# Attention and graph attention on one core: adding two key tiles' weights ahead of the row-sum matmuls between two layers 1

## The chip, the cores and the metric

The kernel runs on one core of one Trainium2 chip. The metric is the device time of that core in microseconds; "the time" is a median of several runs. The engines of the core are TensorE (PE, its weight loads are shown as PEld), VectorE (DVE), ScalarE (ACT), GpSimd (POOL) and SyncE (SP, which issues the DMA transfers). Each works through its own queue of instructions, and they meet through semaphores.

## What is computed

The input is x of 8 batches, 2048 nodes and 256 features in fp32, with one adjacency matrix of 2048 x 2048. Layer 0 is an attention whose softmax is taken over each chunk of 256 keys by itself; the results of the 8 chunks are added. Layer 1 is a graph attention with one score per pair of nodes. Both end in a residual sum and a layer norm.

```python
# layer 0: H = 4 heads of 64, Nc = 8 chunks of 256 keys
scores = einsum('bhnd,bhjcd->bhnjc', q, kc) / sqrt(64)
scores = clip(scores, -10, 10)
scores = where(mask == 0, -10, scores)
attn = softmax(scores, axis=-1)              # over the 256 keys of a chunk
ctx = einsum('bhnjc,bhjcd->bhnd', attn, vc)  # added over the chunks
out = layernorm(ctx @ Wo.T + bo + x) * gamma + beta
x = layernorm(x + out)
# layer 1
e = leaky_relu(s_i[:, :, None] + s_j[:, None, :], 0.2)
attention = softmax(where(mask, e, -inf), axis=-1)
x = layernorm(x + elu(attention @ Wh))
```

## The kernel before

Every order of work is written out by hand. The outer loop goes over `J`, one step for each batch, block of 512 queries and chunk of 256 keys (8 x 4 x 8 = 256 steps). A step has two halves; a half is a *beat* and handles one tile of 128 keys. So layer 0 has 512 beats. In a beat PE makes the scores of four heads in two tiles of PSUM (L899), DVE clips and masks each (L909), and ACT takes the exponential of each into a tile `e` (L912). A chunk leaves four `e` tiles: two key tiles by two pairs of heads.

While chunk J is scored, the chunk before it (`prev`) is multiplied (L922 to L934). There are three passes: part 0 and part 1 are the two halves of each head's 64 features with `v` as weights, and part 2 has a matrix of ones as weights, which gives the softmax sums. Each pass has 2 key tiles x 4 heads = 8 matmuls (16 instructions in the profile), and each head fills 32 of the 128 output rows. The even beat runs parts 2 and 0, the odd beat part 1. ACT copies parts 0 and 1 into `un` (L936) and the sums into `ds` (L942). SP then moves the sums into a small tile `dc` (L944), DVE takes the reciprocal (L950), SP writes it to DRAM (`rd`, L952) and loads it spread over the rows (`r`, L956). Two beats after the sums DVE scales `un` (L963, or L961 for the first chunk), and POOL adds it to `ctxT` (L964). The functions `inverse`, `spread` and `scaled` are put on an `agenda` by the beat in which they are due, and `end_beat` runs them after the generators.

The generators advance by one step in each beat, inside `end_beat`. `fin` is the tail of a layer 0 block: x load, output projection (L357), statistics (L316), the multiplication by gamma and the sum with x (L370, L371), transposes and the store. `prelude` prepares layer 1 of a batch: it makes Wh (L398), key columns and rows, and, for every tile of queries, the maximum over two halves of the keys (`half_max`, L438), then `less_max` and `query_rows`. For the first query block the first four pairs of half maxima take two per beat. `layer1` yields the steps of layer 1: ACT makes the low branch (L714), DVE the leaky maximum (L718) and the mask (L723), ACT the exponential (L727), POOL the running sum (L736), PE the product (L746). `blocks_done` counts finished blocks of layer 1.

Layer 1 of a batch overlaps layer 0 of the next one. Between the last product of one batch's layer 1 and the first step of the next there is a stretch with layer 0, `fin` and `prelude` alone: beats 64 to 88, 134 to 152, 198 to 216 and so on, seven in all. The tiles that the change needs come from the pool `five`, tag `w` (five buffers), which layer 1 uses at other times (L713). The `e` tiles have eight buffers, `ps_m` has two.

Of the kernel before, what the change touches and what calls it, by code (L numbers as in the profile page):

```python
# [19 lines left out]
P = 128  # L20
# [8 lines left out]
def tile_adj_attention__then__gat(  # L29
# [312 lines left out]
    def fin(b, ib, ctxT):  # L342


        xt = one.tile([P, TPB, F], F32, tag="x", name=f"x{b}_{ib}")
        nc.sync.dma_start(out=xt, in_=x[b, ts(ib, IB), :].rearrange("(t p) f -> p t f", p=P))
        yield
        y = one.tile([P, TPB, F], F32, tag="y", name=f"y{b}_{ib}")
        nc.gpsimd.tensor_add(y, xt, bc_rows(bo_bc))  # L349
        nc.gpsimd.tensor_add(xt, xt, bc_rows(beta_bc))  # L350
        while (b, ib) not in ctx_done or ctx_done[b, ib] == beat:
            yield
        for t2 in range(TPB // 2):
            po = ps_m.tile([P, 2, F], F32, tag="m", name=f"po{b}_{ib}_{t2}")
            for j in range(2):
                for k in range(KC):
                    nc.tensor.matmul(  # L357
                        po[:, j, :],
                        ctxT[:, k, ts(2 * t2 + j, P)],
                        WT["o"][:, k, :],  # L360
                        start=(k == 0),
                        stop=(k == KC - 1),
                    )
            nc.vector.tensor_add(y[:, ts(t2, 2), :], po, y[:, ts(t2, 2), :])
        mv, rstd = yield from stats(y, f"a{b}_{ib}")
        yield
        normalize(y, mv, rstd, f"a{b}_{ib}")
        yield
        engine = nc.vector if (b, ib) == (B - 1, NIB - 1) else nc.gpsimd
        engine.tensor_mul(y, y, bc_rows(gamma_bc))  # L370
        engine.tensor_add(y, y, xt)  # L371
        yield
        mv, rstd = yield from stats(y, f"b{b}_{ib}")
        yield
        normalize(y, mv, rstd, f"b{b}_{ib}")
        nc.sync.dma_start(out=h_d[b, ib], in_=y)
        fin_near[b] += 1
        yield
        hT = four.tile([P, KC, IB], F32, tag="xT", name=f"hT{b}_{ib}")
        for k in range(KC):  # L380
            pt = ps_m.tile([P, TPB, P], F32, tag="m", name=f"pt{b}_{ib}_{k}")
            for t in range(TPB):
                nc.tensor.transpose(pt[:, t, :], y[:, t, ts(k, P)], ident)
            nc.scalar.copy(hT[:, k, :], pt.rearrange("p t c -> p (t c)"))
        if (b, ib) == (B - 1, NIB - 1):
            states[b]["hT"] = hT
        else:
            nc.sync.dma_start(out=hT_d[b, ib], in_=hT)
# [70 lines left out]
    def query_rows(m2, name):  # L459
        pt = ps_m.tile([2 * TPB, P], F32, tag="m", name=f"pab{name}")  # L460
        nc.tensor.transpose(pt, m2.rearrange("p n t -> p (n t)"), ident)
        rows = two.tile([2 * TPB, P], F32, tag="rows", name=f"abr{name}")
        nc.scalar.copy(rows, pt)
        ab_d = dram3.tile([2 * TPB, P], F32, tag="ab_d", name=f"ab_d{name}")
        nc.sync.dma_start(out=ab_d, in_=rows)
        return ab_d

    def query_bc(ab_d, name):
        ab = two.tile([P, 2, IB], F32, tag="ab", name=f"ab{name}")
        nc.sync.dma_start(  # L470
            out=ab.rearrange("p n q -> p (n q)"), in_=ab_d.rearrange("r c -> (r c)").partition_broadcast(P)
        )
        return ab

    def prelude(b):


        st = states[b]
        while fin_near[b] < NIB:
            yield  # L480
        hts = [load_hT(b, ib) for ib in range(2)]
        yield
        yield
        while blocks_done < b * NIB:
            yield
        wh = one.tile([P, NT, F + 2], F32, tag="wh", name=f"wh{b}")
        for ib in range(NIB):
            wh_block(b, wh[:, ts(ib, TPB), :], hts[ib], ib)
            if len(hts) < NIB:
                hts.append(load_hT(b, len(hts)))  # L490
            yield
        sj = two.tile([P, 3, NT], F32, tag="sj", name=f"sj{b}")
        key_columns(wh, sj, slice(0, NT))
        yield
        sj_row = one.tile([P, N], F32, tag="sj_row", name=f"sj_row{b}")
        key_rows(b, sj, sj_row, slice(0, NT))
        st["wh"], st["sj"] = [wh[:, ts(ib, TPB), :] for ib in range(NIB)], sj
        fbs, fb_load = far_loads(b, [(it, hf) for it in range(NT) for hf in range(2)])
        yield
        yield  # L500
        for ib in range(NIB):
            m2 = two.tile([P, 2, TPB], F32, tag="m2", name=f"m2{b}_{ib}")
            for n in range(2 * TPB):
                half_max(sj_row[:, ts(n % 2, HN)], fbs.pop(0), m2[:, n % 2, n // 2 : n // 2 + 1])
                fb_load()
                if ib or n % 2:
                    yield
            less_max(sj, ib, m2, f"{b}_{ib}")
            yield
            ab_d = query_rows(m2, f"{b}_{ib}")  # L510
            yield

            while blocks_done < b * NIB + ib - 1:
                yield
            st["ab"][ib] = (beat + 2, query_bc(ab_d, f"{b}_{ib}"))

    def last_prelude(b):

# [291 lines left out]
    def l1_open():  # L810
        return lows or edged or weighted

    def at(when, fn):
        agenda.setdefault(when, []).append(fn)

# [57 lines left out]
    for J in range(total + 1):  # L873
# [5 lines left out]
        for half in range(2):  # L879
# [37 lines left out]
            if prev is not None:  # L917
                if half == 0:

                    pool, tag = (one, "hr") if early and J % 3 == 2 else (two, "un")  # L920
                    prev["un"] = pool.tile([P, 2, IB], F32, tag=tag, name=f"un{prev['name']}")
                for part in ((2, 0), (1,))[half]:  # L922
                    m = ps_m.tile([P, IB], F32, tag="m", name=f"u{prev['name']}_{part}")
                    for i in range(2):
                        pc = 2 * prev["j"] + i
                        for h in range(H):
                            f0 = h * D + part * DH
                            nc.tensor.matmul(  # L928
                                m[h * DH : (h + 1) * DH, :],
                                prev["v"][pc // TPB][:, pc % TPB, f0 : f0 + DH] if part < 2 else ones[:, 0:DH],  # L930
                                prev["es"][2 * i + h // 2][:, h % 2, :],
                                start=(i == 0),
                                stop=(i == 1),
                            )  # L934
                    if part < 2:
                        nc.scalar.copy(prev["un"][:, part, :], m)  # L936
# [36 lines left out]
                        at(beat + 2 + 2 * lag, scaled)  # L973

            end_beat()
            if half == 1:

                if live and j == NCH - 2 and J + 2 < total:
                    nb, nib = (b, ib + 1) if ib + 1 < NIB else (b + 1, 0)
                    xq = xT_tile(nb, nib, "q")  # L980
                if live and j == NCH - 1 and J + 1 < total:
                    qT = make_qT(nb, nib, xq)
# [52 lines left out]
```

## Time and profile before

| what | us |
|---|---|
| median of 3 runs | 4392.91 (4389.68 to 4397.17) |
| the profiled execution's own time | 4387.29 |
| its span, first to last instruction | 4385.5 |
| PE busy | 4064.2 (93%) |
| DVE busy | 3417.7 (78%) |
| ACT busy | 2564.4 (58%) |
| POOL busy | 1760.5 (40%) |

The mean granted clock of TensorE is 0.98. In the lines of the profile, a group has the line of the kernel, the engine, the operation, the tiles as output<-input, partitions x elements, how often it ran, then busy us, mean ns of one, and the idle time of the engine just ahead of it with what ended it. A line of waits has who waited for whom, the total in us, how often, and the longest. A line of the timeline has the start, the length, and what ran; the idle time ahead of it stands in brackets. A line of stretches has start:end and length in us, busy us of each engine with its number of instructions, the granted clock, the busy share of the DMA engines, and GB/s. PE's ends are modelled, and matmuls overlap, so that starts are safer to read than lengths.

### The profile page before, as it was taken

How to read it: one execution, taken by the hardware profiler on the slowest of the kernel's cores; microseconds unless marked ns; L12 is line 12 of the kernel's file. 1: busy time of each engine (PE TensorE's matmuls, PEld its weight loads, DVE VectorE, ACT ScalarE, POOL GpSimd, SP SyncE). 2: the span in 40 equal slices, each digit the busy share in tenths (PEclk: the TensorE clock that was granted, in tenths of full speed). 3: DMA queues.
4: the chain of work that ended last, by engine and by line, in shares of the span. 5: the costliest groups of instructions: out<-in, count | busy, mean ns of one | idle time of the engine just before them, and what ended most of it. 6: DMA issues, size and time to landing. Idle time of an engine off the chain costs nothing. (4 is left out here: it accounts for less than half of the span.)

```text
span 4385.5 us, 61171 instructions
## 1 busy us (share of the span) xinstructions
PE 4064.2 (93%) x23053; PEld 1907.6 (43%) x23053; DVE 3417.7 (78%) x4530; ACT 2564.4 (58%) x3842; POOL 1760.5 (40%) x901
## 2 busy tenths in 40 slices
PE   8889989999999999999899999999999999899767
PEld 3223334454344534454344543445434454344456
DVE  5876589965998669976699766996579965888777
ACT  5655556665566556666566665566556665555546
POOL 0222235543455334444245442554325542354420
PEclk9999999999999999999999999999999999999889
DMA  5554232222332233321333223232232222322321
GB/s 166 182 163 149 71 115 86 83 73 89 99 90 81 64 107 102 100 75 51 105 102 98 74 74 105 85 95 78 70 106 85 89 78 67 115 83 80 123 73 58
DMA packets 257641, 415.63 MB, mean 95 GB/s; under 512 B 85440, under 2 KB 120512, under 8 KB 256448
## 3 DMA queue, kind: packets, MB, share of 16 engines
q1 hardware_dynamic: 257344, 411.71, 30.5%
q8 instruction: 181, 2.97, 0.3%
q14 instruction: 116, 0.95, 0.1%
HBM read 340.66 MB, written 68.88 MB: 93 GB/s over the span
## 5 line engine op out<-in xcount | busy, mean ns | idle before, releaser
L912 ACT ACTIVATE e<-sc 128x1024 f32<-128x1024 f32 x1024 | 1034.2, 1020 | 1049.9 <-DVE sc L909 1006.7
L909 DVE SCALAR_TENSOR_TENSOR sc<-sc,mk 128x1024 f32<-128x1024 f32 x1024 | 1206.7, 1223 | 538.3 <-PE sc L899 352.6
L899 PE MATMUL sc<-qT,kT 64*128 64x512 f32 x4096 | 1060.4, 633 | 86.7 <-ACT e L912 86.2
L964 POOL TENSOR_TENSOR ctxT<-ctxT,un 128x1024 f32<-128x1024 f32 x224 | 568.5, 2538 | 1145.3 <-DVE un L963 1007.0
L928 PE MATMUL u<-e,v 128*32 128x512 f32 x8192 | 980.9, 597 | 0.0
L746 PE MATMUL us<-wh,w 128*128 128x256 f32 x3584 | 878.6, 395 | 81.9 <-ACT w L727 60.4
L746 PEld LDWEIGHTS us<-wh,w 128*128 128x128 f32 x3584 | 667.7, 193 | 422.2 <-ACT w L727 110.7
L736 POOL TENSOR_TENSOR acc<-acc,w 128x512 f32<-128x512 f32 x392 | 601.7, 1535 | 544.9 <-ACT w L727 534.4
L899 PEld LDWEIGHTS sc<-qT,kT 64*128 64x128 f32 x4096 | 347.2, 189 | 611.6 <-ACT e L912 281.8
L718 DVE SCALAR_TENSOR_TENSOR w<-ab,sj,w 128x512 f32<-128x512 f32 x512 | 571.5, 1137 | 4.6 <-ACT w L714 4.5
L928 PEld LDWEIGHTS u<-e,v 128*32 128x32 f32 x8192 | 240.6, 110 | 659.7 <-issue 543.9
L928 PE MATMUL u<-e,ones 128*32 128x512 f32 x4096 | 497.5, 604 | 0.0
L723 DVE TENSOR_TENSOR w<-w,mk 128x512 f32<-128x512 f32 x512 | 458.6, 917 | 37.1 <-DMA mk<-mask 34.6
L438 DVE CUSTOM_DVE_ANT_0 fb<-sj_row,fb 128x1024 bf16<-128x1024 f32 x240 | 387.8, 1626 | 2.3 <-DMA fb<-far 2.3
L714 ACT ACTIVATE w<-ab,sj 128x512 f32<-128x512 f32 x512 | 352.2, 714 | 8.7 <-POOL acc L734 5.4
L727 ACT ACTIVATE w<-w 128x512 f32<-128x512 f32 x512 | 308.8, 629 | 75.9 <-DVE w L723 75.3
L936 ACT COPY un<-u 128x512 f32<-128x512 f32 x512 | 300.5, 587 | 66.5 <-PE u L928 57.6
L963 DVE TENSOR_TENSOR un<-un,r 128x1024 f32<-128x1024 f32 x224 | 278.1, 1242 | 42.2 <-DMA r<-rd 36.7
L928 PEld LDWEIGHTS u<-e,ones 128*32 128x32 f32 x4096 | 107.8, 110 | 356.5 <-issue 305.4
L950 DVE RECIPROCAL dc<-dc 128x16 f32<-128x16 f32 x256 | 63.9, 249 | 149.8 <-DMA dc<-ds 134.0
L942 ACT COPY ds<-u 128x512 f32<-128x512 f32 x256 | 148.5, 580 | 3.0 <-PE u L928 2.5
L349 POOL TENSOR_TENSOR y<-x,bo_bc 128x1024 f32<-128x1024 f32 x32 | 77.6, 2426 | 163.6 <-DMA x<-in_x_dram 103.0
(112 smaller groups left out, 3114.7 us busy)
## 6 DMA issues: line engine op xcount, KB each, us to landing
r<-rd SPq DMA_DIRECT2D x256, 256.0 KB
mk<-mask SPq DMA_DIRECT2D x120, 512.0 KB
fb<-far SPq DMA_DIRECT2D x240, 256.0 KB
xT_k<-in_xT_dram SPq DMA_DIRECT2D x32, 512.0 KB
raw<-in_adjT_dram SPq DMA_DIRECT2D x32, 512.0 KB
rawf<-in_adj_dram SPq DMA_DIRECT2D x32, 512.0 KB
x<-in_x_dram SPq DMA_DIRECT2D x32, 512.0 KB
h_d<-y SPq DMA_DIRECT2D x32, 512.0 KB
```

The source lines that it names most:

```text
L438: nc.vector.tensor_tensor_reduce(out=fb, in0=row, in1=fb, scale=1.0, scalar=2 * FAR * 0.999, op0=ALU.add, op1=ALU.max, accum_out=dst,)
L714: nc.scalar.activation(self.w, k["ab"][:, 1, :], AF.Identity, bias=k["sj"][:, 1, c : c + 1])
L718: nc.vector.scalar_tensor_tensor(self.w, k["ab"][:, 0, :], k["sj"][:, 0, c : c + 1], self.w, ALU.add, ALU.max)
L723: nc.vector.tensor_tensor(self.w, self.w, self.k["mks"][self.c // HT][:, self.c % HT, :], ALU.min)
L727: nc.scalar.activation(self.w, self.w, AF.Exp)
L736: nc.gpsimd.tensor_add(k["acc"], k["acc"], self.w)
L746: nc.tensor.matmul(k["us"][:, t, :], self.w[:, ts(t, P)], k["wh"][c // TPB][:, c % TPB, 0:F], start=(first and t % 2 == 0), stop=last, ski ...
L899: nc.tensor.matmul(sc[:, h, :], kTs[b][c // TPB][h * D : (h + 1) * D, hp, ts(c % TPB, P)], qT[h * D : (h + 1) * D, hp, :], start=True, sto ...
L909: nc.vector.scalar_tensor_tensor(scs[hp], scs[hp], -CLIP, cap, ALU.max, ALU.min)
L912: nc.scalar.activation(e, scs[hp], AF.Exp)
L928: nc.tensor.matmul(m[h * DH : (h + 1) * DH, :], prev["v"][pc // TPB][:, pc % TPB, f0 : f0 + DH] if part < 2 else ones[:, 0:DH], prev["es"] ...
L964: nc.gpsimd.tensor_add(p["ctxT"], p["ctxT"], p["un"])
```

## The change

In the seven stretches, the exponentials of a chunk's two key tiles are added before the sums' matmuls. A new function `l1_rests` says whether layer 1 rests: no step of it is open, its last batch is done, and the prelude of the next batch has not yet sent the rows of its first query block (it sets `near` then). When a chunk's second beat ends and layer 1 rests, POOL adds the two key tiles of heads 0 and 1 (`add_weights(nc.gpsimd, cur, 0)`), each 128 x 512 in fp32; a beat later DVE does the same for heads 2 and 3. For such a chunk, the pass of sums uses the four sums instead of the eight exponentials, so it has 4 matmuls instead of 8, and it stands in the odd beat ahead of part 1, with part 0 alone in the even beat. What follows the sums (copy, transfers, reciprocal, scaling, sum into `ctxT`) comes a beat later with it. In a `fin` block whose L370 and L371 fall into such a stretch, these two run on DVE instead of POOL. The first query block of a batch's layer 1 starts a beat later if its start would be even.

```diff
--- before.py
+++ after.py
@@ -366,7 +366,7 @@
         yield
         normalize(y, mv, rstd, f"a{b}_{ib}")
         yield
-        engine = nc.vector if (b, ib) == (B - 1, NIB - 1) else nc.gpsimd
+        engine = nc.vector if (b, ib) == (B - 1, NIB - 1) or l1_rests() else nc.gpsimd
         engine.tensor_mul(y, y, bc_rows(gamma_bc))
         engine.tensor_add(y, y, xt)
         yield
@@ -508,11 +508,14 @@
             less_max(sj, ib, m2, f"{b}_{ib}")
             yield
             ab_d = query_rows(m2, f"{b}_{ib}")
+            st["near"] = True
             yield
 
             while blocks_done < b * NIB + ib - 1:
                 yield
-            st["ab"][ib] = (beat + 2, query_bc(ab_d, f"{b}_{ib}"))
+
+            start = beat + 2
+            st["ab"][ib] = (start + (ib == 0 and start % 2 == 0), query_bc(ab_d, f"{b}_{ib}"))
 
     def last_prelude(b):
 
@@ -809,6 +812,19 @@
 
     def l1_open():
         return lows or edged or weighted
+
+    def l1_rests():
+
+        if not 2 * NIB * NCH <= beat < 2 * total or l1_open() or leaking:
+            return False
+        return blocks_done % NIB == 0 and "near" not in states[blocks_done // NIB]
+
+    def add_weights(engine, chunk, hp):
+
+        for h in range(2):
+            w2 = five.tile([P, IB], F32, tag="w", name=f"w2{chunk['name']}_{hp}_{h}")
+            engine.tensor_add(w2, chunk["es"][hp][:, h, :], chunk["es"][2 + hp][:, h, :])
+            chunk["w2"].append(w2)
 
     def at(when, fn):
         agenda.setdefault(when, []).append(fn)
@@ -919,18 +935,20 @@
 
                     pool, tag = (one, "hr") if early and J % 3 == 2 else (two, "un")
                     prev["un"] = pool.tile([P, 2, IB], F32, tag=tag, name=f"un{prev['name']}")
-                for part in ((2, 0), (1,))[half]:
+                added = prev.get("w2")
+                for part in (((0,), (2, 1)) if added else ((2, 0), (1,)))[half]:
                     m = ps_m.tile([P, IB], F32, tag="m", name=f"u{prev['name']}_{part}")
-                    for i in range(2):
+                    summed = part == 2 and added
+                    for i in range(1 if summed else 2):
                         pc = 2 * prev["j"] + i
                         for h in range(H):
                             f0 = h * D + part * DH
                             nc.tensor.matmul(
                                 m[h * DH : (h + 1) * DH, :],
                                 prev["v"][pc // TPB][:, pc % TPB, f0 : f0 + DH] if part < 2 else ones[:, 0:DH],
-                                prev["es"][2 * i + h // 2][:, h % 2, :],
+                                added[h] if summed else prev["es"][2 * i + h // 2][:, h % 2, :],
                                 start=(i == 0),
-                                stop=(i == 1),
+                                stop=(i == 1 or bool(summed)),
                             )
                     if part < 2:
                         nc.scalar.copy(prev["un"][:, part, :], m)
@@ -973,6 +991,11 @@
                         at(beat + 2 + 2 * lag, scaled)
 
             end_beat()
+            if prev is not None and half == 0 and "w2" in prev:
+                add_weights(nc.vector, prev, 1)
+            if live and half == 1 and l1_rests():
+                cur["w2"] = []
+                add_weights(nc.gpsimd, cur, 0)
             if half == 1:
 
                 if live and j == NCH - 2 and J + 2 < total:
```

## The prediction

> **What bounds the kernel now.** I read the page's busy shares first, then its groups, then stretches, waits and timeline of one pause between two layers 1. Busy shares and groups:
>
> ```profile
> PE 4064.2 (93%) x23053; PEld 1907.6 (43%) x23053; DVE 3417.7 (78%) x4530; ACT 2564.4 (58%) x3842; POOL 1760.5 (40%) x901
> ...
> L909 DVE SCALAR_TENSOR_TENSOR sc<-sc,mk 128x1024 f32<-128x1024 f32 x1024 | 1206.7, 1223 | 538.3 <-PE sc L899 352.6
> ...
> L736 POOL TENSOR_TENSOR acc<-acc,w 128x512 f32<-128x512 f32 x392 | 601.7, 1535 | 544.9 <-ACT w L727 534.4
> ...
> L438 DVE CUSTOM_DVE_ANT_0 fb<-sj_row,fb 128x1024 bf16<-128x1024 f32 x240 | 387.8, 1626 | 2.3 <-DMA fb<-far 2.3
> ...
> L928 PE MATMUL u<-e,ones 128*32 128x512 f32 x4096 | 497.5, 604 | 0.0
> ```
>
> PE at 93% makes a saved matmul look like saved time. But a share is an average; the change acts in seven pauses only. So, a pause (beats 262 to 279) in three stretches; columns are length, then busy us of PE, PEld, DVE, ACT, POOL:
>
> ```profile
> 2065.60:2087.40 21.80, 20.90 (x147) 7.18 (x146) 17.88 (x34) 17.11 (x26) 13.58 (x7) 1.00 0.37 120
> 2087.40:2138.30 50.90, 47.11 (x269) 21.27 (x265) 18.44 (x21) 26.60 (x45) 7.06 (x3) 1.00 0.28 85
> 2138.30:2189.60 51.30, 43.98 (x275) 14.75 (x274) 44.25 (x67) 23.64 (x32) 20.58 (x9) 0.97 0.34 109
> ```
>
> The middle stretch, where Wh (L398) is made, is PE's: DVE works 18 of 51 us. The last, with the half maxima (L438), is DVE's: 44 of 51 us, and its 7 idle us are waits on DMA, PE and POOL. The waits and the timeline (start, us) show two couplings:
>
> ```profile
> DVE dc L950 <- DMA dc<-ds: 134.0, 98, 4.7
> ```
> ```profile
> 2139.54 2.36 DVE L909 SCALAR_TENSOR_TENSOR sc<-sc,mk 128x1024 f32<-128x1024 f32 x2 [6.45 <-ACT qT L257]
> 2145.40 0.25 DVE L950 RECIPROCAL dc<-dc 128x16 f32<-128x16 f32 x1 [2.38 <-DMA dc<-ds]
> 2145.57 2.34 DVE L909 SCALAR_TENSOR_TENSOR sc<-sc,mk 128x1024 f32<-128x1024 f32 x2
> 2147.82 1.22 DVE L438 CUSTOM_DVE_ANT_0 fb<-sj_row,fb 128x1024 bf16<-128x1024 f32 x1
> 2148.95 3.38 DVE L438 CUSTOM_DVE_ANT_0 fb<-sj_row,fb 128x1024 bf16<-128x1024 f32 x1
> ```
> ```profile
> 2140.22 1.93 PE L928 MATMUL u<-e,ones 128*32 128x512 f32 x16
> 2141.96 1.90 PE L928 MATMUL u<-e,v 128*32 128x512 f32 x16
> 2143.79 1.99 PE L899 MATMUL sc<-qT,kT 64*128 64x512 f32 x8
> ```
> ```profile
> 2147.87 3.38 POOL L350 TENSOR_TENSOR x<-x,beta_bc 128x1024 f32<-128x1024 f32 x1
> 2151.21 3.35 POOL L964 TENSOR_TENSOR ctxT<-ctxT,un 128x1024 f32<-128x1024 f32 x1
> ```
>
> First: after the sums, the reciprocal waits for a DMA round trip and ends 6.0 us after that beat's clip began (2139.54 to 2145.57); the next clip stands behind it, though PE had begun the next scores at 2143.79. Second: a half maximum that takes 1.22 us alone took 3.38 with a GpSimd operation beside it, which itself took 3.38.
>
> [...] The clip has one operand in PSUM and shows no such stretching (1223 ns). [...] the trace has 0.69 us for 128x512 adds (L364), and 0.60 from start to start. [...] the trace's 1.27 is used. [...]
>
> **The change, part by part.** By the built order, it takes in 65 chunks (11 in the first pause, 9 in each of six). Layer 1 starts in the same beats as before, since the new parity term meets odd starts only: nothing there.
>
> *PE, removed.* Eight of 16 instructions of a sums pass. A pass starts 1.74 us before the next (2140.22 to 2141.96): 0.87 us a chunk, 65 x 0.87 = 56.6 us at most.
>
> *DVE, added.* Two adds a chunk in the even beat, 0.60 each: 1.2 us. They stand ahead of the next beat's clip.
>
> *POOL, added.* Two adds a chunk after the second key tile's exponential, 1.27 each: 2.5 us. POOL is 40% busy and its own time is hidden[...].
>
> *Moved to DVE.* The gamma and x operations (L370, L371) of seven fin blocks: about 1.15 each from start to start against 2.36 on POOL. In the pause shown they meet 2.38 us of DVE idle ahead of the clip at 2066.83: nothing, 2.3 us a block if that cover is gone.
>
> *Moved a beat.* The sums' copy, the dc, rd and r transfers, reciprocal, scaling and ctxT add go from even to odd beats. SP's issues keep their order within a chunk; the first fin block's x load moves a beat past the r load. Its output projection now follows a beat later.
>
> *Waits added.* The sums wait for both engines' adds; behind them on PE stand u part 1 and the next scores. The five w tiles make the second POOL add and both DVE adds wait for the previous chunk's sums, which stand a beat earlier: nothing, unless PE lags.
>
> **A pair of beats, worked out.** From a scores pass at t: clip from t+1.24, first exponential done 2.32 after the clip's start, reciprocal done 6.0 after it. Before, an even beat is 5.49 on PE, an odd one 3.77: 9.26. But the odd clip begins at 7.24, behind the reciprocal, its exponential is done at 9.56, and only that frees the scores buffer. So a bare pair takes 9.56 (the one at 2138.3: 5.49+4.10 = 9.59). Afterwards PE has 8.39, but the reciprocal now closes the odd beat of 4.64: next clip at 7.24, exponential at 9.56. Again 9.56: a bare pair gains nothing. PE time counts only where a beat holds other PE work.
>
> *First stretch.* Clip of 262 at 2066.83; two clips 2.3, statistics 2.3, row sums 0.3, scaling 1.15 and now the adds 1.2 end near 2074.1, against 2073.55 for the next clip before. That odd beat's reciprocal ends 6.0 later, so 264's clip starts at 2080.2 (was 2077.90); statistics and adds again, 2086.0 for 265's (2084.87); its first exponential at 2088.3 and PE's own 2.6 after the adds let beat 266 start at 2088.7 (2087.39): 1.3 late.
>
> *Middle stretch.* From beat 266 on, five even beats lose a pass and the odd ones gain half of one, but Wh's second tile waits for the copy of u (two PSUM buffers; that copy stands behind the beat's exponentials, which 265's reciprocal holds). Beat 267 starts at 2099.0 (2096.76), 268 at 2107.9 (2106.33), 270 at 2124.7 (2123.51), 272 at 2138.2 (2138.30), 273 at 2142.0 (2143.79): from 1.3 late to 1.8 ahead, 3.1 regained.
>
> *Last stretch.* DVE bound. Adds of three chunks, 3 x 1.2 = 3.6. Locks: three POOL pairs, fully met 3 x 2.54 = 7.6, none if they fall under clips; half maxima, adds and scaling queue there, so I take two thirds, 5.1. L370 and L371, which block the small maxima now (L453 1.07 and L455 2.21 us instead of 0.15), move a beat: -1.9, the rest meeting other work. Sum +6.8.
>
> A pause: 1.3 - 3.1 + 6.8 = +5.0; seven: +35 us. Bounds of a pause: no lock and L370's relief whole (+3.6 - 3.0), saving kept: -1 to -2; all locks met and no relief: +9.5. The profiled execution took 4387.3 us (span 4385.5, 1.8 around it), 5.6 below the runs' median of 4392.9. 4387.3 + 35 = 4422; at the median **4428 us**, 0.8% slower.
>
> **The rivals.**
>
> *PE is the bound throughout: faster.* For it: 93% busy. Against: PE stands 7.3 us in the last stretch and bare pairs run at the DMA loop. All 56.6 us would give 4336; more likely a part, 10 to 40 us (4350 to 4380), if POOL's adds fall under clips and the moved operations save stalls. It decides as soon as DVE's extra in the last stretch stays under the 1.8 us gained ahead of it. Chance 0.25.
>
> *A wash.* Extra and saving cancel: 4393, within 0.2% (8.8 us, about what measurement tells from no change). Chance 0.08.
>
> *The lock dominates: clearly slower.* Every POOL add meets a DVE operation, and late POOL adds hold the sums and all of PE behind them: +9.5 to 11 a pause, +66 to +77, about 4465. For it: 3.38 us for 1.22 above. Against: DVE idles 32 us of the middle stretch. Chance 0.12.
>
> *It doesn't happen.* Excluded by the built order.
>
> **How the numbers follow.** My case (4405 to 4455) has 0.55; with the lock's 0.12, slower has 0.67; same 0.08, faster 0.25. The range 4360 to 4465 leaves out the deep end of the faster case and the lock's upper tail.
>
> **What would show it.** Right: sums passes of half length in 65 chunks, no shorter bare pairs; the last stretch longer by 5 us or more, with half maxima and new adds at 1.8 to 2.5 us beside POOL adds; reciprocals waiting in odd beats; 4096-520 matmul instructions on ones. Wrong: a last stretch no longer than before, new POOL adds at 1.27 with DVE's adds at 0.69, and middle stretches shorter by 3 us or more. What would make it wrong is above all how often a POOL add meets a two-input DVE operation, which no row of before counts for these times.

## The result and the profile after

The changed kernel takes 4497.15 us (median of 4 runs, 4495.44 to 4498.61), the kernel before 4395.04 (4389.68 to 4399.45) beside it: a ratio of 1.0239, 95% interval 1.0219 to 1.0258, or +102 us. The forecast had the direction; 4428 and its range, 4360 to 4465, did not hold the time.

The page of the changed kernel, busy shares and groups (lines of the changed kernel's code: L915 are the scores, L925 the clip, L946 the products, L954 and L960 the copies of `u` and of the sums, L968 the reciprocal, L970 and L974 the rd and r transfers, L981 the scaling, L982 the sum into `ctxT`, L826 the new adds):

```profile
PE 4088.8 (91%) x22533; PEld 1923.7 (43%) x22533; DVE 3572.1 (79%) x4674; ACT 2565.9 (57%) x3842; POOL 1927.6 (43%) x1017
...
L438 DVE CUSTOM_DVE_ANT_0 fb<-sj_row,fb 128x1024 bf16<-128x1024 f32 x240 | 387.4, 1624 | 1.5 <-DMA fb<-far 1.3
L946 PE MATMUL u<-e,ones 128*32 128x512 f32 x3056 | 371.3, 604 | 0.0
...
L968 DVE RECIPROCAL dc<-dc 128x16 f32<-128x16 f32 x256 | 63.7, 249 | 199.5 <-DMA dc<-ds 199.0
L826 POOL TENSOR_TENSOR w<-e,e 128x512 f32<-128x512 f32 x130 | 198.7, 1549 | 23.8 <-ACT e L928 23.7
```

PE runs 520 instructions fewer, as built, and yet is busy 24.6 us longer than before (4064.2). The half maxima cost what they cost before (1626 ns then). The groups by line show the other new work:

```profile
L826 DVE TENSOR_TENSOR w<-e,e 128x512 f32<-128x512 f32 x130 | 124.5, 998 | 0.0
L946 PE MATMUL u<-w,ones 128*32 128x512 f32 x520 | 121.8, 663 | 38.2 <-DVE w L826 19.7 <-POOL w L826 18.4
...
L371 DVE TENSOR_TENSOR y<-y,x 128x1024 f32<-128x1024 f32 x8 | 17.4, 2176 | 0.3
```

The waits for the sums' transfer grew from 134.0 to 199.0 us, and PE now waits ahead of the transposes of `fin` for a copy of `u`, a wait that its list before did not have:

```profile
DVE dc L968 <- DMA dc<-ds: 199.0, 109, 5.4
...
PE pt L383 <- ACT un L954: 53.0, 14, 5.7
```

The same three stretches of the same pause (beats 262 to 265, 266 to 271, 272 to 279; columns as before):

```profile
2124.40:2150.23 25.83, 22.32 (x131) 7.85 (x130) 21.99 (x38) 17.92 (x26) 14.12 (x8) 0.93 0.37 115
2150.23:2202.73 52.50, 47.52 (x246) 22.35 (x242) 22.24 (x28) 25.90 (x45) 18.83 (x12) 0.93 0.23 70
2202.73:2261.28 58.55, 46.28 (x244) 15.06 (x243) 52.11 (x64) 23.73 (x32) 27.90 (x14) 0.88 0.33 100
```

They last 25.83, 52.50 and 58.55 us; before it was 21.80, 50.90 and 51.30. The forecast made its cut one beat later, at the start of beat 273, which puts beat 272 (3.77 us, 5.49 before) into the middle: so cut, the three are +4.0, -0.1 and +8.9, where the forecast had +1.3, -3.1 and +6.8. PE's granted clock, the column after POOL, fell from 1.00, 1.00 and 0.97 to 0.93, 0.93 and 0.88. After the pause come +6.3 us in beats 280 to 283, of which 1.8 come back by beat 292. All seven pauses together explain about 110 of the 111.3 us between the two profiled spans (4385.5 and 4496.8); outside them the beats are as long as before.

Three places of this pause, from the timeline (start, length; idle time ahead of it in brackets). The first is beat 274, at the start of the half maxima:

```profile
2202.13 0.33 SPq L421 DMA_DIRECT2D sj_row<-sj_d  x1
2202.52 0.90 SPq L430 DMA_DIRECT2D fb<-far  x2
2203.46 0.46 SPq L970 DMA_DIRECT2D rd<-dc  x1
...
2208.29 0.55 SPq L974 DMA_DIRECT2D r<-rd  x1
...
2215.51 1.22 DVE L981 TENSOR_TENSOR un<-un,r 128x1024 f32<-128x1024 f32 x1 [3.13 <-DMA r<-rd]
2218.31 0.25 DVE L968 RECIPROCAL dc<-dc 128x16 f32<-128x16 f32 x1 [1.57 <-DMA dc<-ds]
...
2220.86 3.78 PE L915 MATMUL sc<-qT,kT 64*128 64x512 f32 x8 [5.79 <-ACT e L928]
```

A beat later than before, rd and r come behind the transfers of the key rows (`sj_row`) and the far tiles (`fb`) on SP's queue, and r is issued 4.8 us after rd (1.4 us before, from 2145.68 to 2147.10). Scaling, reciprocal and clip follow one another late, and PE stands 5.79 us. Then its eight matmuls take 3.78 us instead of 1.99. The view of stretches, for that pass alone, has the granted clock (the column after POOL):

```profile
2220.86:2224.60 3.74, 3.74 (x8) 1.13 (x8) 3.74 (x3) 1.01 (x1) 3.74 (x2) 0.50 0.40 122
```

The granted clock is 0.50, where it was 1.00 in the pass of 1.99 us before. This pass is not alone: all 12 scores' passes in the changed kernel that follow an idle time of 3 us or more (3.36 to 6.26) spread their starts over 2.73 us, at granted clocks of 0.50 to 0.57; without idle time the median is 1.40, at 1.00. In the kernel before, 4 of 5 such passes do; the fifth, after 3.02 us, has 1.88.

The second place is in the next beat, where DVE and GpSimd operations stand beside each other:

```profile
2222.59 3.35 DVE L438 CUSTOM_DVE_ANT_0 fb<-sj_row,fb 128x1024 bf16<-128x1024 f32 x1
2224.82 3.91 POOL L826 TENSOR_TENSOR w<-e,e 128x512 f32<-128x512 f32 x2
...
2225.87 3.41 DVE L826 TENSOR_TENSOR w<-e,e 128x512 f32<-128x512 f32 x2
...
2227.12 3.28 PE L946 MATMUL u<-w,ones 128*32 128x512 f32 x5 [2.48 <-POOL w L826]
```

The half maximum stands beside the `ctxT` sum on GpSimd (2221.54 to 2224.86) and takes 3.35 us; the 150 half maxima of this profile that have no GpSimd instruction beside them take 1.21 us at the median, 1.23 at most. Beside each other GpSimd's two adds then take 3.91 us and DVE's two 3.41; with nothing of the other engine beside it, one takes 1.27 us on GpSimd and 0.68 on DVE at the median. PE waits for the adds. This stretching is what the prediction and the expectations call the lock or the exclusion. The clip does not show it: 605 of its 1024 instructions have a GpSimd instruction beside them, and none takes more than 1.23 us. The third is the way out of the pause, beat 281, where a delayed chunk's reciprocal and a normal chunk's stand in successive beats (279 and 280):

```profile
2273.78 0.25 DVE L968 RECIPROCAL dc<-dc 128x16 f32<-128x16 f32 x1 [4.04 <-DMA dc<-ds]
...
2277.87 1.11 PE L383 MATMUL pt<-ident,y 128*128 128x128 f32 x4 [5.39 <-ACT un L954]
...
2278.91 3.79 PE L915 MATMUL sc<-qT,kT 64*128 64x512 f32 x8
```

The clip stands behind the reciprocal, the exponentials behind the clip, the copy of `u` behind them, and the transposes behind that copy. PE stands 5.39 us, and the scores' pass at 2278.91 takes 3.79 us, at a granted clock of 0.50.

### The profile page after: what moved, and what is told of

Read it like the earlier page. It is cut to its first block, busy times and chain, and to the rows that moved or that the text cites. A ratio compares the mean times of both kernels' runs of the same rounds, so it can differ in the third digit from the quotient of the medians.

```text
span 4496.8 us, 60359 instructions
## 1 busy us (share of the span) xinstructions
PE 4088.8 (91%) x22533; PEld 1923.7 (43%) x22533; DVE 3572.1 (79%) x4674; ACT 2565.9 (57%) x3842; POOL 1927.6 (43%) x1017
## 4 chain that ended last, share of the span: by engine, by line
PE 59%; DVE 25%; issue 6%; ACT 5%; DMA 4%; POOL 1%; SPq 0%; DVEq 0%; POOLq 0%; ACTq 0%
PE u L946 16%; PE sc L915 15%; PE us L749 14%; DVE sc L925 10%; PE pw L398 3%; PE pq L256 3%; PE pk L256 3%; DVE fb L438 3%; PE pv L275 2%; DVE w L721 2%; DMA dc<-ds 2%; PE po L357 2%; DVE w L726 2%; ACT e L928 2%; PE us L764 1%
## 5 line engine op out<-in xcount | busy, mean ns | idle before, releaser
L925 DVE SCALAR_TENSOR_TENSOR sc<-sc,mk 128x1024 f32<-128x1024 f32 x1024 | 1206.2, 1222 | 513.0 <-PE sc L915 362.0
L915 PE MATMUL sc<-qT,kT 64*128 64x512 f32 x4096 | 1076.0, 643 | 94.3 <-ACT e L928 93.9
L982 POOL TENSOR_TENSOR ctxT<-ctxT,un 128x1024 f32<-128x1024 f32 x224 | 571.0, 2549 | 1122.7 <-DVE un L981 1077.5
L946 PE MATMUL u<-e,v 128*32 128x512 f32 x8192 | 1011.0, 598 | 0.0
L915 PEld LDWEIGHTS sc<-qT,kT 64*128 64x128 f32 x4096 | 357.4, 193 | 617.7 <-issue 273.2
L721 DVE SCALAR_TENSOR_TENSOR w<-ab,sj,w 128x512 f32<-128x512 f32 x512 | 590.0, 1173 | 6.2 <-ACT w L717 6.1
L946 PEld LDWEIGHTS u<-e,v 128*32 128x32 f32 x8192 | 253.1, 110 | 652.9 <-issue 525.8
L946 PE MATMUL u<-e,ones 128*32 128x512 f32 x3056 | 371.3, 604 | 0.0
L954 ACT COPY un<-u 128x512 f32<-128x512 f32 x512 | 301.3, 588 | 76.3 <-PE u L946 47.5
L981 DVE TENSOR_TENSOR un<-un,r 128x1024 f32<-128x1024 f32 x224 | 275.6, 1231 | 16.3 <-DMA r<-rd 15.8
L968 DVE RECIPROCAL dc<-dc 128x16 f32<-128x16 f32 x256 | 63.7, 249 | 199.5 <-DMA dc<-ds 199.0
L826 POOL TENSOR_TENSOR w<-e,e 128x512 f32<-128x512 f32 x130 | 198.7, 1549 | 23.8 <-ACT e L928 23.7
L946 PEld LDWEIGHTS u<-e,ones 128*32 128x32 f32 x3056 | 80.3, 110 | 269.6 <-issue 218.5
L398 PE MATMUL pw<-W_aug,hTl 128*128 128x258 f32 x496 | 135.4, 426 | 39.7 <-ACT un L954 30.5
```

Of the source, the lines that this page charges most:

```text
L721: nc.vector.scalar_tensor_tensor(self.w, k["ab"][:, 0, :], k["sj"][:, 0, c : c + 1], self.w, ALU.add, ALU.max)
L915: nc.tensor.matmul(sc[:, h, :], kTs[b][c // TPB][h * D : (h + 1) * D, hp, ts(c % TPB, P)], qT[h * D : (h + 1) * D, hp, :], start=True, sto ...
L925: nc.vector.scalar_tensor_tensor(scs[hp], scs[hp], -CLIP, cap, ALU.max, ALU.min)
L946: nc.tensor.matmul(m[h * DH : (h + 1) * DH, :], prev["v"][pc // TPB][:, pc % TPB, f0 : f0 + DH] if part < 2 else ones[:, 0:DH], added[h] i ...
L982: nc.gpsimd.tensor_add(p["ctxT"], p["ctxT"], p["un"])
```

## The experiments

Each time is a median, with the difference to the kernel before in runs on the same chip. Diffs are against the changed kernel, unless they say otherwise. "L370/L371 back" means that these two are on GpSimd again, as before.

### The parts, one at a time

The delay alone, L370/L371 back:

```diff
-for part in (((0,), (2, 1)) if added else ((2, 0), (1,)))[half]:
+for part in (((0,), (2, 1)) if "w2" in prev else ((2, 0), (1,)))[half]:
-    add_weights(nc.vector, prev, 1)
-    add_weights(nc.gpsimd, cur, 0)
```

> Nothing is added: in the same 65 chunks the pass of sums keeps its 8 matmuls and only moves to the odd beat, with its copy, transfers, reciprocal, scaling and ctxT add; gamma and x stay on POOL. Theory D (the delay costs: the reciprocal's DMA wait now stands ahead of the clips of even beats, r meets the key rows' transfers, and transposes and Wh wait for copies behind the held exponentials): +60 to +130 us on before, the bulk of the +102 that the whole change cost. Theory L (the adds and the lock between DVE and POOL cost): within 15 us of before.

Measured: 4433.75 us, ratio 1.0093 (1.0078 to 1.0108), +42, between the ranges of the two theories. Both waits that grew in the changed kernel are there without any add:

```profile
DVE dc L968 <- DMA dc<-ds: 192.0, 109, 5.1
PE pt L383 <- ACT un L954: 51.2, 14, 5.3
```

The adds alone, unread, L370/L371 back:

```diff
-added = prev.get("w2")
+added = None
```

> The adds run on POOL and DVE where the change has them, but nobody reads them: sums stay in the even beat with 8 matmuls; gamma and x stay on POOL. Theory L: +60 to +100 us on before. Theory D: +10 to +40, for 1.2 us of DVE and the lock in the half maxima's stretch, seven times.

Measured: 4528.55, ratio 1.0314 (1.0294 to 1.0334), +137: more than the whole change, and more than either theory had. Only the move of L370/L371 undone:

```diff
-engine = nc.vector if (b, ib) == (B - 1, NIB - 1) or l1_rests() else nc.gpsimd
+engine = nc.vector if (b, ib) == (B - 1, NIB - 1) else nc.gpsimd
```

> The changed kernel with the gamma and x operations back on POOL. The first stretch lost 4.0 us in the pause looked at, of which the DVE x operation, 2.18 us beside a POOL add, is a part. If the move costs, 1 to 3 us a pause come back: 4476 to 4490. If the move was a relief, up to +15: 4512. Theories D and L do not differ here.

Measured: 4495.07, ratio 1.0230 (1.0215 to 1.0246), +103: the move is worth nothing that can be told, neither the cost nor the relief expected. The delay undone and the adds kept and used, with both engines' adds at the end of the odd beat, L370/L371 back:

```diff
-for part in (((0,), (2, 1)) if added else ((2, 0), (1,)))[half]:
+for part in (((0, 2), (1,)) if added else ((2, 0), (1,)))[half]:
-if prev is not None and half == 0 and "w2" in prev:
-    add_weights(nc.vector, prev, 1)
     add_weights(nc.gpsimd, cur, 0)
+    add_weights(nc.vector, cur, 1)
```

> Half-length sums without the delay: both engines add at the end of the chunk's odd beat, and the pass stands in the even beat behind part 0; gamma and x stay on POOL. Theory D: most of the loss is gone, between -30 and +25 us on before. Theory L: the same adds and locks remain, +40 to +90 us.

Measured: 4517.62, ratio 1.0280 (1.0264 to 1.0295), +126. That is above both theories. So the delay is not the whole of it. The adds stand at another place here, right behind the exponentials that they read: DVE waits 41.6 us for `e` ahead of its adds, and PE 51.5 us for GpSimd's.

### Whose adds cost, and where they stand

GpSimd's adds alone, then DVE's alone, both unread (`added = None`), L370/L371 back, and then all four on DVE in the changed kernel:

```diff
# GpSimd's alone
-    add_weights(nc.vector, prev, 1)
# DVE's alone
-    add_weights(nc.gpsimd, cur, 0)
# all on DVE (the passes' order stays that of the changed kernel)
+    add_weights(nc.vector, prev, 0)
     add_weights(nc.vector, prev, 1)
-    add_weights(nc.gpsimd, cur, 0)
```

> GpSimd's two adds per chunk alone, at their place after the second key tile; nothing reads their results, the sums' pass is the full one in its old beat, and L370/L371 stay on GpSimd. The adds on DVE are left out. Theory A (DVE's adds cost by their place on DVE's queue, ahead of the next clip, so that their own time and what stretches them is paid): GpSimd's adds alone cost little, 0 to +30 us against the kernel before. Theory B (GpSimd's new adds cost[...]): most of the +137 of the run with both adds stays, +60 to +110 us, with half maxima and DVE's L371-like operations stretched beside L826 on POOL.

Measured: 4417.12, ratio 1.0056 (1.0040 to 1.0071), +24.

> DVE's two adds per chunk alone, at their place behind the scaling in the even beat; unread, the sums' pass is the full one in its old beat, L370/L371 stay on GpSimd. GpSimd's adds are left out. Theory A (their place on DVE's queue; the ctxT add that the scaling releases on GpSimd stretches them): +90 to +140 us against before, and DVE's L826 pairs of 3 us and more remain beside L982 on POOL. Theory B (GpSimd's adds cost by exclusion): +20 to +60 us, and DVE's pairs fall to about 1.2 us.

Measured: 4498.09, ratio 1.0236 (1.0220 to 1.0252), +105.

> The changed kernel with all four adds of a chunk on DVE, in one place, behind the even beat's scaling; GpSimd makes none. The sums' pass is the half-length one in the odd beat, as in the changed kernel. Theory A (place and time on DVE's queue): slower than the changed kernel, by 65 chunks x 1.2 us = 78 us if all of it is paid, so +60 to +90 us against it (+160 to +190 against before). Theory B (exclusion by GpSimd's adds): faster than the changed kernel, +40 to +80 us against before.

Measured: 4530.26, ratio 1.0310 (1.0295 to 1.0326), +137, 35 above the changed kernel: theory A in sign, at half its size. The timeline of the run with DVE's adds alone shows what the +105 are:

```profile
2127.22 0.24 DVE L968 RECIPROCAL dc<-dc 128x16 f32<-128x16 f32 x1
2127.38 2.85 POOL L982 TENSOR_TENSOR ctxT<-ctxT,un 128x1024 f32<-128x1024 f32 x1 [0.78 <-DVE un L981]
2127.38 3.40 DVE L826 TENSOR_TENSOR w<-e,e 128x512 f32<-128x512 f32 x2
...
2130.70 2.35 DVE L925 SCALAR_TENSOR_TENSOR sc<-sc,mk 128x1024 f32<-128x1024 f32 x2
```

The pair stands behind the reciprocal, ahead of the next clip, and beside the `ctxT` sum that the scaling had just released; it takes 3.40 us where two adds take 1.28 alone (at 2206.25 in the changed kernel). All of it delays the clip. If that is right, the same adds ahead of the scaling and the reciprocal run while DVE would wait for dc anyway:

```diff
# against the run with DVE's adds alone
+if prev is not None and half == 0 and "w2" in prev:
+    add_weights(nc.vector, prev, 1)
 end_beat()
-if prev is not None and half == 0 and "w2" in prev:
-    add_weights(nc.vector, prev, 1)
```

> DVE's two adds a chunk alone, unread, as in the run with DVE's adds alone (+105 us), but ahead of all that the even beat's end issues, so ahead of the reciprocal that waits for dc, not behind it; sums, GpSimd's operations and L370/L371 as before the change. Theory R (work behind the reciprocal's wait is paid whole, work ahead of it runs while it waits): 0 to +40 us against before. Theory Q (their time and the exclusions are the price): +80 to +120 us.

Measured: 4423.63, ratio 1.0054 (1.0037 to 1.0071), +24 instead of +105. Its group of adds:

```profile
L826 DVE TENSOR_TENSOR w<-e,e 128x512 f32<-128x512 f32 x130 | 85.1, 695 | 0.0
```

695 ns instead of 1257, and off the way to the clip. The edit changes two things: the adds no longer stand behind the wait for dc, and they no longer meet the `ctxT` sum. The pair is 1.1 us shorter, 73 us in 65 chunks, of the 81 us gained; no run parts the two. The same edit in the changed kernel, and with both engines' adds unread:

> The changed kernel with DVE's adds moved ahead of all that the even beat's end issues (statistics, half maxima, and the reciprocal in the beat that enters or leaves a pause); everything else as in the changed kernel. If their place matters here as it did for DVE's adds alone (+105 behind the reciprocal, +24 ahead of it): 30 to 70 us faster than the changed kernel. If it matters only behind the reciprocal's wait, which in the changed kernel stands in the odd beat: within 15 us of the changed kernel. In both cases slower than before by at least the delay's 41 less what PE saves.

Measured: 4507.04, ratio 1.0248 (1.0232 to 1.0263), +110: no gain there, since the changed kernel's reciprocal stands in the odd beat and its adds were not behind it.

> Both engines' adds, unread, DVE's ahead of what the even beat's end issues, GpSimd's at their place; sums in full and in their old beat, L370/L371 on GpSimd. If the adds' prices just add up: 24 + 24 = +48 us against before, +40 to +60. If GpSimd's and DVE's adds hold each other up on top of that: +70 to +110 us, with DVE's L826 well above the 0.69 us it takes without GpSimd's.

Measured: 4460.24, ratio 1.0147 (1.0130 to 1.0163), +63, just above one theory's bracket and just below the other's: 24 + 24, and 15 that would be what the two engines' adds do to each other (DVE's mean is 962 ns here, 695 without GpSimd's).

### Where in the pause

The changed kernel, with each pause's adds ended before the half maxima:

```diff
 key_rows(b, sj, sj_row, slice(0, NT))
+st["near"] = True
```

> The changed kernel with each pause's adds ended before the half maxima: 37 chunks instead of 65 (7 in the first pause, 5 in each other). If the loss sits by place (in the changed kernel's pause shown: entry +4.0, half maxima +8.9, exit +6.3 of which 1.9 comes back), the half maxima's part goes and entry and exit stay: 7 x (4.0 + 4.4) = +59, so +45 to +75 us against before, with the exit's two reciprocals in successive beats now at beats 271 and 272. If it goes with the number of chunks: 102 x 37/65 = +58, the same sum, but then spread over the beats; the trace decides: the place theory has the half maxima's beats within 2 us of before. If the half maxima themselves make all of the loss, it is gone: -10 to +20 us.

Measured: 4473.42, ratio 1.0177 (1.0158 to 1.0195), +80, a little over the bracket. In the pause shown, beats 274 to 279 take 43.6 us, 41.7 before, just within the 2 us of the place theory, and the way out moved with its two successive reciprocals (beats 271 and 272): beats 273 and 274 take 7.75 and 8.90 us instead of 4.10 and 6.71.

```profile
2203.27 0.25 DVE L969 RECIPROCAL dc<-dc 128x16 f32<-128x16 f32 x1 [7.14 <-DMA dc<-ds]
...
2205.76 3.79 PE L916 MATMUL sc<-qT,kT 64*128 64x512 f32 x8 [3.91 <-ACT e L929]
```

The normal chunk's dc is issued at 2197.76, right behind the delayed chunk's r, which itself comes 5.3 us after its rd; from dc's issue to its reciprocal it takes 5.5 us, where the pair of beats in the kernel before had 1.9 (2143.46 to 2145.40). So leaving a pause costs 5.8 us here, where nothing of layer 1 is near, and 0.3 of it comes back. Taking four chunks' adds and delay out of each pause's half maxima gave 22 us in all.

### Moving the reciprocal

In the next three runs a summed chunk's reciprocal and transfers stand a beat later, so that DVE finds dc there: in the changed kernel; without any adds or delay and with L370/L371 back; and in the changed kernel with DVE's adds first.

```diff
-at(beat + lag, inverse)
-at(beat + lag, spread)
+late = int("w2" in prev)
+at(beat + lag + late, inverse)
+at(beat + lag + late, spread)
```

> The changed kernel, but a summed chunk's reciprocal and its transfers to and from DRAM stand one beat later (the even beat after the sums), so that DVE finds dc there; the scaling stays where it is. Theory R (DVE waits in its own beat for the sums' transfer, and everything behind that wait is late: in the changed kernel it holds the even beats' clips, so PE's shorter passes never show): faster than the changed kernel by 0.6 to 1.5 us for each of the 65 chunks, 40 to 100 us, so 4395 to 4455 us, with waits of dc falling from 199 us to below 120. Theory Q (DVE's added time and the exclusions are the price, wherever they stand): within 15 us of the changed kernel.

Measured: 4529.45, ratio 1.0297 (1.0281 to 1.0312), +130.

> The kernel before without any adds, with full sums in their old beat; in the pauses alone the reciprocal and its transfers stand one beat later than before, the scaling where it was. Theory R: bare pairs are no longer held by the round trip (9.56 against 9.26 on PE), and Wh's second tile not by the copy of u behind it: 10 to 60 us faster than before. Theory Q: within 10 us of before. Against both: if the later r transfer comes too late for the scaling, DVE waits for r in the even beat, and it is slower by up to 2 us for each of 65 chunks.

Measured: 4544.61, ratio 1.0331 (1.0316 to 1.0347), +145.

> The changed kernel with the reciprocal and its transfers one beat later and DVE's adds ahead of all that the even beat's end issues. Theory R: another 5 to 40 us faster than the run with the later reciprocal alone, near or below the kernel before (4370 to 4410 us), if PE's shorter passes now show. Theory Q: within 15 us of the changed kernel.

Measured: 4573.41, ratio 1.0397 (1.0382 to 1.0413), +174. Theory R failed with this remedy: all three are slower. The waits of the run without adds tell where the wait went:

```profile
DVE un L981 <- DMA r<-rd: 233.2, 40, 8.9
...
DVE dc L968 <- DMA dc<-ds: 68.4, 62, 4.6
```

The wait for dc halved (134.0 before), and the scaling now waits 233.2 us for r (36.7 before). Sums to scaling is one chain of three transfers in two beats, and these runs find no beat to spare in it; where a later part of it is pushed, DVE stands there.

### The shorter passes by themselves

Delay and well placed adds are 42 + 63 = 105 already, which leaves nothing for the shorter passes. So these alone: in the 65 chunks the sums leave out the second key tile, without adds, once in the old beat, once in the delayed one; L370/L371 back.

```diff
# the adds are left out; order of the passes: first run as before, second as in the delay alone
-summed = part == 2 and added
+summed = part == 2 and "w2" in prev
-    added[h] if summed else prev["es"][2 * i + h // 2][:, h % 2, :],
+    prev["es"][2 * i + h // 2][:, h % 2, :],
```

> The half-length sums' passes alone: in the 65 chunks the pass leaves out the second key tile (the sums then cover the first key tile only) and has 4 matmuls; no adds, sums in their old beat, L370/L371 on GpSimd. If PE bounds the pauses: 35 to 56 us faster than before (65 x 0.87 = 56.6). If the reciprocal's round trip, DVE and PSUM bound most beats: 5 to 30 us faster, since the sums still end 0.87 us earlier.

Measured (12 runs): 4394.54, ratio 0.9998 (0.9989 to 1.0007), -1. Half of the sums' matmuls in 65 chunks, for nothing, and below both ranges of gain expected.

> The same half-length passes (the second key tile left out of the sums), but in the odd beat as in the changed kernel; no adds, L370/L371 on GpSimd. Beside the run with the delay alone (+41 against before): if the shorter passes bring nothing once they are delayed, within 10 us of it, +30 to +50; if PE's time counts, 0.87 us for each of 65 chunks less, -15 to +5 against before.

Measured: 4429.42, ratio 1.0080 (1.0060 to 1.0101), +34, 8 below the delay alone, with intervals that overlap. The page and the timeline of the first of the two, bare pair of beats 272 and 273:

```profile
PE 4018.0 (91%) x22533; PEld 1893.6 (43%) x22533; DVE 3411.6 (78%) x4530; ACT 2562.4 (58%) x3842; POOL 1763.3 (40%) x901
```
```profile
2154.29 1.06 PE L946 MATMUL u<-e,ones 128*32 128x512 f32 x8
...
2154.87 2.15 ACT L928 ACTIVATE e<-sc 128x1024 f32<-128x1024 f32 x2 [1.70 <-DVE sc L925]
2156.92 0.58 ACT L960 COPY ds<-u 128x512 f32<-128x512 f32 x1
...
2159.81 0.25 DVE L968 RECIPROCAL dc<-dc 128x16 f32<-128x16 f32 x1 [2.72 <-DMA dc<-ds]
...
2162.30 2.26 PE L915 MATMUL sc<-qT,kT 64*128 64x512 f32 x8 [1.46 <-ACT e L928]
```

The sums end on PE by 2155.4. Their copy stands behind the two exponentials on ScalarE and starts at 2156.92, when these end. From there the transfer, the reciprocal, the next clip and its exponential run as before, and PE gives the saved time back as 1.46 us of waiting. In the kernel before the order was the same, and there the sums ended at 2142.15, 0.7 us ahead of their copy (beats 272 and 273):

```profile
2140.80 2.16 ACT L912 ACTIVATE e<-sc 128x1024 f32<-128x1024 f32 x2 [1.71 <-DVE sc L909]
2142.86 0.58 ACT L942 COPY ds<-u 128x512 f32<-128x512 f32 x1
```

The test is to put the copy ahead of the second exponential, in the same 65 chunks' even beats, once with the short passes and once with full ones:

```diff
-for hp in range(NPAIR):
+def exponential(hp):
     e = eight.tile(...)
     nc.scalar.activation(e, scs[hp], AF.Exp)
     cur["es"].append(e)
+held = half == 0 and prev is not None and "w2" in prev
+exponential(0)
+if not held:
+    exponential(1)
...
 nc.scalar.copy(ds, m)
+if live and held:
+    exponential(1)
```

> The half-length passes in their old beat (the sums leave out the second key tile), without adds, and in these 65 chunks ScalarE copies the sums ahead of the even beat's second exponential, not behind it. If the place of the copy behind the exponentials is what hides the shorter passes: the reciprocals come up to 1 us earlier, 10 to 60 us faster than with the half-length passes alone. If PE, DVE or the scores' buffers set the beats anyway: within 10 us of them; slower by up to 0.6 us a chunk (+39) if the later second exponential holds the next scores instead.

Measured: 4359.69, ratio 0.9930 (0.9914 to 0.9947), -33, where the short passes alone had -1.

> The kernel before with full sums and no adds, and in the same 65 chunks the sums' copy on ScalarE ahead of the even beat's second exponential. The full sums end about 1.3 us after the first exponential begins to be due, so the copy waits for PE: 0 to +40 us against before on every theory; less gain than with the half-length passes, by 10 us or more, if these only show once the copy is not behind the exponentials.

Measured: 4371.09, ratio 0.9954 (0.9939 to 0.9969), -21. This is the kernel before with one copy moved in 65 beats, with its full sums, and it beats both kernels; the expectation gave it no gain. Its bare pair (beats 272 and 273):

```profile
2136.46 1.02 ACT L928 ACTIVATE e<-sc 128x1024 f32<-128x1024 f32 x1 [1.71 <-DVE sc L925]
2137.91 0.58 ACT L965 COPY ds<-u 128x512 f32<-128x512 f32 x1 [0.43 <-PE u L951]
...
2140.78 0.26 DVE L975 RECIPROCAL dc<-dc 128x16 f32<-128x16 f32 x1 [2.10 <-DMA dc<-ds]
...
2143.27 2.26 PE L915 MATMUL sc<-qT,kT 64*128 64x512 f32 x8
```

The copy even waits 0.43 us for PE's full pass behind the first exponential, and two beats on the scores follow without a wait: the pair lasts 9.31 us (2133.96 to 2143.27), against 9.59 before and 9.26 of PE work. With the copy there, the short passes are worth 11 us (4371.09 - 4359.69); with it behind the exponentials, 1. That the copy's place hides a part of what the passes save is thus shown. Why the rest of the 56.6 us stays away is not shown; the traces suggest DVE's queue in the first stretch and in the half maxima.

## Why the prediction went wrong

Four runs nest, each with one part more, so that their differences give each part behind the ones ahead of it: the delay alone +42; with the shorter passes +34; with the adds, read by the sums, +103; with the move, the whole change, +102. The prediction's terms for seven pauses, beside what they measured (differences of runs on several chips, good to a few us):

| term | forecast | measured |
|---|---|---|
| the delay (in "first stretch", 1.3 a pause, with the adds that stand there) | +9 | +42 |
| shorter passes ("middle stretch", 3.1 a pause) | -22 | -8 |
| adds and locks ("last stretch", 3.6 + 5.1 a pause) | +61 | +69 |
| L370 and L371 on DVE ("last stretch", 1.9 a pause) | -13 | -1 |
| sum | +35 | +102 |

**"Moved a beat": the failed step that cost most.** The delay was put at 1.3 us a pause and costs 6. The profiled run of the delay alone has +3.7, -1.5, +4.0 for the three stretches of the pause shown and +2.6 for the way out, 1.8 of which comes back. I had followed the reciprocal's wait into the odd beats, and the SP queue within a chunk; I had not followed rd and r past the key rows' transfers (beat 274), nor the last delayed chunk into the first normal one (beat 281). The way out was in no sum at all.

**"Middle stretch", 3.1 us regained a pause: failed.** The 22 us in all are 1 by themselves and 8 behind the delay. (The step counts five even beats from 266 on; up to its end at beat 273 there are four.) That a bare pair gains nothing held: beats 272 and 273 take 9.93 us with the short passes alone, 9.59 before. In the changed kernel these two took 8.49, and the beat behind them 9.64 instead of 6.71. But the 6.0 us that the prediction took as the round trip of the sums' transfer include the copy's wait behind the second exponential: with the copy ahead of it, the pair with full passes takes 9.31. And I let PE's time count "where a beat holds other PE work". In the pause shown it does not there either: with the short passes alone PE waits 0.90 us for the copy of the sums ahead of Wh's first tile, and Wh's second tile waits for the copy of `u` as long as before, 1.80 us (first line) and 1.84 (second, the kernel before):

```profile
2116.19 4.57 PE L398 MATMUL pw<-W_aug,hTl 128*128 128x258 f32 x12 [1.80 <-ACT un L954]
```
```profile
2103.51 2.88 PE L398 MATMUL pw<-W_aug,hTl 128*128 128x258 f32 x12 [1.84 <-ACT un L936]
```

Beats 266 and 267 take 20.6 us there, 18.9 before; that difference is in these matmuls, 4.57 us instead of 2.88. The rival "PE is the bound throughout" falls with the 1 us: PE at 93% had 520 instructions too many, and no time to win by leaving them out alone.

**The adds and their locks: right in size, in part by luck.** The 61 us stood for three chunks of each last stretch; the 5.1 of the locks was an estimate, two thirds of the 7.6 us that three pairs of GpSimd adds take at 1.27 each (the shortest L736 of the profile before). The run with everything but the move and the one with the delay and the shorter passes differ by +0.5, -0.5 and +5.0 us in the three stretches of the pause shown and by +1.8 on the way out, so its last stretch has 5.0 of the 8.7 forecast, and other pauses have up to 14.3 in all. And the price was not a property of the adds: unread and without the delay they cost 137 as the change places them and 63 with DVE's ahead of the reciprocal.

**L370 and L371: the relief of 1.9 a pause did not come.** Undoing the move changes the time by 2 us or less. On DVE, L371 meets the new GpSimd adds and takes 2.18 us on average instead of the 1.15 that the step had.

**What the sum had no term for: PE's rate.** The changed kernel and the run with the short passes alone have the same 22533 PE instructions; PE is busy 4088.8 us in one and 4018.0 in the other. Of the 102.0 us between their spans (4496.8 and 4394.8), 70.8 are PE busy for longer with as many instructions (granted clock 0.963 and 0.978 on average) and 31.2 are PE idle. In the seven pauses PE stands still for more than 2.5 us 31 times after the change, 17 times with the short passes alone, and 7 times before. In the changed kernel the granted clock over the 3.7 us behind such a stall is 0.50 to 0.62 in 30 of the 31 places, and 1.00 in one. At 1.8 us more in the pass behind such a stall (3.78 for 1.99 above), the 14 stalls more are an estimate of 25 of the 70.8 us. This is a count, not an experiment: what makes up the rest, and how much of it lay on the path, stays open.

**The rivals.** The clearly slower one named 4465 by the lock alone; the time went past it, by other means. Of the signs named, half-length passes in 65 chunks and a last stretch longer by 5 us or more came true.

## What to carry to other kernels

Before pricing a saving on the busiest engine, take that work out alone and look whether the time moves: at 93% busy, half a pass in 65 chunks was worth 1 us, and where a beat was looked at, it closed over clip, exponential, copy, transfer and reciprocal. In such a loop look for small instructions queued behind large ones that they don't need (one copy ahead of one exponential: 21 us), and put new work ahead of an instruction that waits, not behind it (24 us instead of 105; the adds then no longer met a GpSimd operation either, and took 695 ns on average instead of 1257). When a chain is moved by a beat, follow its last member into the first that isn't moved, and each of its transfers past what its queue holds there.

## What the hardware showed that was not expected

- After 5.79 us without work, PE ran a scores' pass at a granted clock of 0.50, in 3.78 us for 1.99: 1.8 us on top of the stall itself.
- Two DVE adds of 128 x 512 took 3.40 us beside one GpSimd add of 128 x 1024, which took 2.85, and 1.28 alone. Such a GpSimd add takes 2.36 us at the median with no DVE instruction beside it (12 of the 224 in the changed kernel); the two lengths add up to 3.64.
- A reciprocal that finds its input ready is no gain if the transfer after it then comes late: 134.0 us of waiting for dc became 68.4, and 36.7 for r became 233.2.
